# Layer 0 of block 1 by two levels of a Winograd scheme, with the residual in its weights

## The chip, the cores and the metric

The kernel runs on one core of a Trainium2 chip. The metric is the device time of one execution in microseconds (us). TensorE multiplies, VectorE (DVE), ScalarE (ACT) and GpSimd (POOL) do the elementwise work, and SP issues nearly all DMAs; each engine works through its own queue in order.

## The reference

Four layers act on x of 8 sequences x 256 tokens x 1024 features in fp32, each with a residual and each with low-rank adapters (rank 16) that are picked for every sequence by an index. The change concerns the first:

```python
base_out = jnp.einsum('bti,oi->bto', x, W) + b
A = lora_As[adapter_mapping]
Bm = lora_Bs[adapter_mapping]
lora_h = jnp.einsum('bti,bir->btr', x, A)
lora_out = jnp.einsum('btr,bro->bto', lora_h, Bm)
return base_out + lora_out * SCALING        # SCALING = 2
...
x = x + _L0_cond_ref(x, ...)                # residual around layer 0
x = x + _L1_cond_ref(x, ...)                # gate, up, silu(gate) * up, down (F = 2752)
x = x + _L2_cond_ref(x, ...)                # low rank alone
x = x + _L3_cond_ref(x, ...)
```

## The kernel before

**Tiling.** Tokens lie along the free dimension, features along the 128 partitions. The 2048 tokens are two blocks of 1024 (`blk`), each in two halves of 512 (`n`). Layer 0 runs for both blocks first, `layer0(0)` and `layer0(1)`; then for each block gate and up (`gate_up`) and the rest (`down_projection`). What layer 0 gives, x1, is stored to memory (`x1d`) and read again as the residual of layer 1.

**One level and two.** All large products save multiplications by Winograd's form of Strassen's scheme: a 2x2 product of blocks takes seven products of sums of blocks. Layer 0 uses one level: `job(o)` (L894) makes two of the eight output chunks from seven products with 512 columns (`product`, L372), with sums of weights (`sum_w`) and of tokens (`sum_x`) on DVE. Its first quarter in block 0 is `plain` (L865), with no scheme. `with_bias` (L849) evicts a product from PSUM and adds bias and residual x. Gate and up use two levels, `Quads` (L385): 7 steps x 7 blocks, a block being 2 x 2 matmuls with 256 columns in `step` (L464). The outer sums of the tokens, and the inner ones, are made once per block by `prepare_tokens` (L656): DVE and ACT make them from x1, and for each half of the features (`kk`) they are stored to memory (`toks`, 7 places of 7 x 256 columns) and read back for every group of gate and up, two tiles a step (`load_tok`, L419). The weights' outer sums (`outer`, L431) and inner ones (`inner_sums`, L439) are POOL's. A block's products leave PSUM by ACT copies or DVE additions.

**The order of the work.** A list of units (a job, a step) is emitted in turn; each has slots, and between slots things hung on it are emitted: `u.before(k, slot, f)` puts f at a slot of the unit k before it, `u.at(slot, f)` at its own. Light work goes to a queue `beside`, from which each slot takes items until their costs reach the unit's share (1.3 for a layer-0 job, `SHARE` for a step). `need(key)` empties that queue until something is ready. The last block of a step is kept back (`pending`) until slot 2 of the next. The tile framework then orders the instructions of each engine from this, so that a ready load can go ahead of a waiting store.

**Buffers.** Nearly all tiles of 8 KB per partition come from one pool of 22 (`big`, L119), in program order: x, sums, weights, tokens, results.

**Beside the change.** After block 0's jobs, `finished` (L857) stores x1 and puts block 0's token preparation beside block 1's jobs. `SumDown` (L755) loads a slice of the down weights, sums it on POOL and stores the sums (2.1 MB in all each): four of them in block 1's last layer-0 job, four in block 0's groups of gate and up. The first part of gate and up is the remainder (`rest`, L1099), 7 steps of half the width, whose tokens are loaded two units ahead; then five full groups (`job`, L998). A group's low-rank part is four matmuls of 32 rows for each finished result (`expand_gu`, L987).

Of the kernel before, what the change touches and what calls it, by code (L numbers as in the profile page):

```python
# [8 lines left out]
F32 = mybir.dt.float32  # L9
I32 = mybir.dt.int32  # L10
# [7 lines left out]
NB = 8  # L18
S = 256
R = 16  # L20
SLOTS1 = 16
SLOTS2 = 64
TB = 1024
# [31 lines left out]
def kernel(  # L55
# [3 lines left out]
    toks_in: bass.AP,  # L59
    w0: bass.AP,  # L60
    w0a: bass.AP,
    b0: bass.AP,
    a0: bass.AP,
    bb0: bass.AP,
    wgu: list,
    wrem: bass.AP,
    wd2: bass.AP,
# [44 lines left out]
    tpool = ctx.enter_context(tc.tile_pool(name="t", bufs=2))  # L112
# [6 lines left out]
    def big(name):  # L119
        return upool.tile([P, BIG], F32, tag="u", name=name)  # L120

    def bank(pool, name):
        return pool.tile([P, 512], F32, tag=pool.name, name=name)
# [91 lines left out]
    along = const.tile([P, 32], I32, tag="along", name="along")  # L215
    nc.gpsimd.iota(along, pattern=[[1, 32]], base=0, channel_multiplier=0)
    pick = const.tile([P, 32], F32, tag="pick", name="pick")
    nc.vector.tensor_copy(pick, along)
    nc.vector.tensor_scalar(pick, pick, place_f, None, op0=ALU.is_equal)
# [5 lines left out]
    nc.vector.tensor_single_scalar(  # L225
        off_gx[:, :, 1, :], off_gx[:, :, 1, :], 4.0 * R * SLOTS1, op=ALU.add
    )


    def gather(t, table, off):  # L230
# [154 lines left out]
    class Quads:  # L385


        deep = 2
        columns = (1, 0)

        def __init__(self, blk, name, nq, load_raw, done, share):
            self.blk, self.name, self.nq = blk, name, nq
            self.load_raw, self.done = load_raw, done
            self.raw, self.sums, self.tok, self.c = {}, {}, {}, {}
            self.units = []
            for s in range(len(ORDER)):
                u = Unit(f"{name}_{s}", lambda at, s=s: self.step(s, at), share[ORDER[s]])
                u.before(2 if nq == 1 else 1, 0, lambda s=s: self.load_tok(s))
                u.before(1, 1, lambda s=s: self.inner_sums(s))
                self.units.append(u)  # L400
            first = self.units[0]
            first.before(3, 0, lambda: (self.load("B11"), self.load("B12")))
            first.before(2, 0, lambda: self.load("B22"))
            first.before(1, 0, lambda: self.load("B21"))
            self.units[0].at(2, lambda: self.outer("T3", "B22", "B12", "sub"))
            self.units[1].at(3, lambda: self.outer("B12", "B12", "B11", "sub"))
            self.units[2].at(2, lambda: self.outer("B11", "T3", "B11", "add"))
            self.units[4].at(2, lambda: self.outer("B21", "B21", "B11", "sub"))
# [147 lines left out]
    class Down(Quads):  # L556
# [92 lines left out]
            return weights, tokens  # L649


    toks = [
        dram.tile([7, 2, P, 7 * S], F32, tag=f"toks{b}", name=f"toks{b}") for b in range(NBLK)
    ]

    def prepare_tokens(blk, kk, h):  # L656

# [123 lines left out]
    def layer0(blk):  # L781
# [75 lines left out]
        def finished(kk):  # L857
            for n in range(NN):
                nc.sync.dma_start(
                    out=x1d[blk][n, kk], in_=st["x1", n, kk].rearrange("p i c t -> p (i c t)")  # L860
                )
            if blk == 0:
                beside.extend(prepare_tokens(blk, kk, [st["x1", n, kk] for n in range(NN)]))

        def plain(o, at):  # L865

# [27 lines left out]
        def job(o, at):  # L894
# [33 lines left out]
            more(p, 1, pl)  # L928
            at(7)

        for i, o in enumerate((0, 2, 1, 3)):
            if blk == 0 and i == 0:
                u = Unit("0_plain", lambda at, o=o: plain(o, at), 0)
                u.before(1, 0, load_x)
                for c in range(HC):
                    u.before(1, 0, lambda c=c: sum_x(c))
            else:
                u = Unit(f"0_{blk}_{o}", lambda at, o=o: job(o, at), 1.3)
                u.before(1, 0, lambda o=o: load_w(o))
                u.before(1, 3, lambda o=o: sum_w(o))  # L940
                if i == 0:
                    u.before(1, 0, load_x)
                    for c in range(HC):
                        u.before(1, 4 + c // 2, lambda c=c: sum_x(c))
                    u.at(4, first_shrink)
            if i % 2:
                u.at(8, lambda kk=o % 2: finished(kk))
            if blk == 1 and i == 3:
                for c in range(4):
                    w = SumDown(c)  # L950
                    u.at(2 * c - 2 if c else 0, w.load)
                    u.at(2 * c, w.sums)
                    u.at(2 * c + 3, w.store)

    def gate_up(blk):
        st = sts[blk]
# [41 lines left out]
        def job(g):  # L998
# [91 lines left out]

            q = Quads(blk, f"1_{blk}_{g}", 2, raw, done, SHARE)
            q.units[0].before(3, 0, lambda: tables(g))
            if blk == 0 and g < KQ:
                w = SumDown(g + 4)
                q.units[2].at(0, w.load)
                q.units[2].at(5, w.sums)
                q.units[4].at(0, w.store)
# [94 lines left out]
    def down_projection(blk):  # L1192
# [200 lines left out]
        def last_layers():  # L1393


            x2, t, banks = st["x2"], {}, []
            final = blk + 1 == NBLK
            if final:
                spare = big("spare").rearrange("p (j t) -> p j t", j=4)

            def ranks(n):
                rows = slice(64 * n, 64 * n + 64)
                t[n] = tpool.tile([P, 512], F32, tag="t", name=f"t23_{blk}_{n}")
                nc.vector.tensor_mul(t[n][rows], st.pop(("p23", n))[rows], mask[rows])

            def store(o, n):
                at = blk * TB + n * 512

                queue_of = nc.sync if final else nc.scalar
                if final and n == 1 and o in TAIL:  # L1410
                    queue_of = nc.gpsimd
                queue_of.dma_start(out=outT[o * P : (o + 1) * P, at : at + 512], in_=x2[o][n])

            def products(*which):
                pss = []
                for o, n in which:
                    banks.append(None)
                    ps = bank((ps_l, ps_a)[len(banks) % 2], f"p23_{blk}_{o}_{n}")
                    expand(ps, st["a23"], o, t[n], 64 * n, 64 * n + 64, start=True)
                    pss.append(ps)  # L1420
                for (o, n), ps in zip(which, pss):
                    if final and n == 1 and o in TAIL:

                        copy(spare[:, TAIL.index(o)], ps)
                        nc.gpsimd.tensor_add(x2[o][n], x2[o][n], spare[:, TAIL.index(o)])
                        store(o, n)
                        continue
                    nc.vector.tensor_add(x2[o][n], x2[o][n], ps)

                    if final:  # L1430
                        store(o, n)
                    else:
                        beside.append((0.2, lambda o=o, n=n: store(o, n)))

            for c in (HC - 1, NC - 1):
                shrink_half(c, 1)
            shrink_half(HC - 1, 0)
            ranks(1)
            if final:
# [12 lines left out]
            ranks(0)  # L1452
            if not final:
                products((2, 1))
            for o in range(NC - ahead):
                products((o, 0), (o + ahead, 1))
            for o in range(NC - ahead, NC):
                products((o, 0))
# [31 lines left out]
                u.at(6, table_a)  # L1490
        units[-1].at(9, last_layers)

    for blk in range(NBLK):
        layer0(blk)
    for blk in range(NBLK):
        gate_up(blk)
        down_projection(blk)
# [149 lines left out]
```

## Time and profile before

| | |
|---|---|
| time, median of 3 runs | 1804.67 us (1803.13 to 1806.73) |
| the profiled execution | 1805.19 us, span 1803.4 us |
| TensorE | 1790.4 us busy, 99% of the span |
| DVE, ACT, POOL | 1051.5, 298.6, 984.1 us busy |
| DMA | 403.38 MB, 224 GB/s over the span |
| layer 0, block 0 | 0 to 119.3 us, DMA share 0.62 |
| layer 0, block 1 | 119.3 to 227.7 us, DMA share 0.77 |
| remainder of gate and up, block 0 | 227.7 to 273.1 us, DMA share 0.98 |

The span runs from the first to the last instruction; the execution's time has some 1.8 us around it. Lines are named by the engine that worked, the tile written and the line of the kernel (L476 is the matmul of a two-level step, L375 that of a one-level product). fp32 matmuls appear as two instructions each. The DMA share is the part of the time in which the 16 DMA engines were busy, on average.

### The profile page before, as it was taken

The page shows a single profiled execution, that of the slowest core. Times are in us where ns is not written, and L with a number is a line of the kernel's source. Part 1 is how long each engine was busy: PE and PEld are TensorE (multiplying, and loading weights), DVE is VectorE, ACT ScalarE, POOL GpSimd, SP SyncE. Part 2 cuts the span into 40 slices and gives each one's busy share as a digit, 9 for nine tenths or more (in the row PEclk, how much of TensorE's full clock was granted, in tenths as well). Part 3 has the DMA queues.
Part 4 walks back from the last instruction along what each step waited for, and adds up shares of the span by engine and source line. Part 5 has one row for each costly group of instructions (what it writes and reads, how often), then busy time and mean ns, then how long its engine had stood idle before and what let it go on. Part 6 is the DMA issues. An engine that isn't in the chain of part 4 may idle for free.

```text
span 1803.4 us, 20672 instructions
## 1 busy us (share of the span) xinstructions
PE 1790.4 (99%) x7664; PEld 1312.2 (73%) x7664; DVE 1051.5 (58%) x1675; ACT 298.6 (17%) x536; POOL 984.1 (55%) x742
## 2 busy tenths in 40 slices
PE   9999999999999999999999999999999999999998
PEld 4444477888787878788854678787888887888743
DVE  5584255666666666748842464757575758554623
ACT  0121023020202121224210031121212121221000
POOL 6202579685868686344530567676767564443301
PEclk9999999999999999999999999999999999999999
DMA  6476895867676755778831865575848475745302
GB/s 233 172 281 250 273 396 184 304 225 287 215 294 208 298 187 217 260 272 311 316 135 67 307 264 192 176 292 171 296 165 290 166 256 184 255 165 180 110 0 94
DMA packets 119094, 403.38 MB, mean 224 GB/s; under 512 B 11858, under 2 KB 42706, under 8 KB 109522
## 3 DMA queue, kind: packets, MB, share of 16 engines
q1 hardware_dynamic: 108752, 382.24, 58.4%
q0 software_dynamic: 6080, 12.99, 2.3%
q10 hardware_dynamic: 4162, 6.82, 1.2%
q8 instruction: 62, 1.02, 0.2%
q14 instruction: 38, 0.31, 0.0%
HBM read 317.59 MB, written 84.41 MB: 223 GB/s over the span
## 4 chain that ended last, share of the span: by engine, by line
PE 93%; DVE 3%; issue 2%; DMA 1%; POOL 0%; ACT 0%; DVEq 0%; POOLq 0%; ACTq 0%; SPq 0%
PE pa L476 26%; PE pc L476 13%; PE pa_d L476 11%; PE pa L375 10%; PE pb L476 6%; PE pc_d L476 5%; PE pc L375 5%; PE pb_d L476 3%; PE pb L375 2%; PE pl L989 2%; PE pa_r L476 2%; PE pp L875 2%; PE pd L261 1%; PE pc_r L476 1%; DMA w_B<-in_wgu_dram 1%
## 5 line engine op out<-in xcount | busy, mean ns | idle before, releaser
L476 PE MATMUL pa<-tk,sw 128*128 128x256 f32 x1120 | 268.9, 383 | 1.7 <-DVE c_X L507 1.7
L476 PE MATMUL pc<-tk,sw 128*128 128x256 f32 x1120 | 264.9, 379 | 0.3 <-POOL sw L447 0.3
L476 PEld LDWEIGHTS pa<-tk,sw 128*128 128x128 f32 x1120 | 209.0, 190 | 59.9 <-issue 10.6
L476 PEld LDWEIGHTS pc<-tk,sw 128*128 128x128 f32 x1120 | 212.5, 190 | 31.2 <-issue 1.8
L476 PE MATMUL pa<-tk,w_B 128*128 128x256 f32 x960 | 227.8, 380 | 0.0
L476 PEld LDWEIGHTS pa<-tk,w_B 128*128 128x128 f32 x960 | 181.6, 190 | 32.5 <-issue 6.5
L446 POOL TENSOR_TENSOR sw<-w_B 128x512 f32<-128x512 f32 x60 | 76.5, 1275 | 170.8 <-PE pa L476 151.3
L614 POOL TENSOR_TENSOR dx_d<-dw_d 128x1024 f32<-128x1024 f32 x14 | 33.0, 2356 | 164.7 <-PE pa L476 44.3
L476 PE MATMUL pb<-tk,w_B 128*128 128x256 f32 x480 | 113.4, 379 | 0.0
L476 PE MATMUL pa_d<-dh_d,dw_d 128*128 128x256 f32 x448 | 102.2, 379 | 0.0
L476 PE MATMUL pc_d<-dh_d,dw_d 128*128 128x256 f32 x448 | 101.7, 379 | 0.0
L476 PEld LDWEIGHTS pb<-tk,w_B 128*128 128x128 f32 x480 | 91.2, 190 | 12.4
L507 DVE TENSOR_TENSOR c_X<-c_X,pa 128x512 f32<-128x512 f32 x90 | 61.5, 683 | 64.9 <-PE pa L476 64.9
L437 POOL TENSOR_TENSOR w_B<-w_B,w_B 128x1024 f32<-128x1024 f32 x40 | 93.4, 2356 | 2.4 <-PE pa L476 2.4
L476 PEld LDWEIGHTS pa_d<-dh_d,dw_d 128*128 128x128 f32 x448 | 85.0, 190 | 12.4 <-issue 0.8
L476 PEld LDWEIGHTS pc_d<-dh_d,dw_d 128*128 128x128 f32 x448 | 85.0, 190 | 12.4 <-issue 0.8
L448 POOL TENSOR_TENSOR sw<-w_B 128x512 f32<-128x512 f32 x60 | 87.8, 1463 | 0.0
L449 POOL TENSOR_TENSOR sw<-w_B,sw 128x512 f32<-128x512 f32 x60 | 80.6, 1343 | 3.9
L447 POOL TENSOR_TENSOR sw<-sw,w_B 128x512 f32<-128x512 f32 x60 | 76.9, 1282 | 0.0
L286 ACT ACTIVATE c_X<-pa 128x512 f32<-128x512 f32 x30 | 17.7, 591 | 341.1 <-PE pa L476 341.1
L231 POOL DMA_INDIRECT ad<-in_ad_dram,off_a x48 | 46.1, 961 | 31.3 <-PE pd L261 20.9
L375 PE MATMUL pa<-ht,wd 128*128 128x512 f32 x128 | 60.2, 600 | 0.0
(380 smaller groups left out, 3118.1 us busy)
## 6 DMA issues: line engine op xcount, KB each, us to landing
tk<-toks SPq DMA_DIRECT2D x140, 896.0 KB, 6.6
w_B<-in_wgu_dram SPq DMA_DIRECT2D x40, 1024.0 KB, 5.0
tk_r<-toks SPq DMA_DIRECT2D x28, 896.0 KB, 11.0
hk<-c_Z SPq DMA_DIRECT2D x32, 512.0 KB, 4.1
dh_d<-hk SPq DMA_DIRECT2D x14, 1024.0 KB, 8.4
hk<-c_Y SPq DMA_DIRECT2D x24, 512.0 KB, 4.1
x1d<-x SPq DMA_DIRECT2D x8, 1024.0 KB, 6.4
wo<-in_wd_dram SPq DMA_DIRECT2D x8, 1024.0 KB, 7.0
```

The source lines that it names most:

```text
L231: nc.gpsimd.indirect_dma_start(out=t, out_offset=None, in_=table, in_offset=bass.IndirectOffsetOnAxis(ap=off, axis=0),)
L375: nc.tensor.matmul(ps, v[j], m[j], start=start and k == 0, stop=k == len(moving) - 1, skip_group_check=True,)
L437: f(self.raw[out][:, c], self.raw[a][:, c], self.raw[b][:, c])
L446: nc.gpsimd.tensor_add(s1, m21, m22)
L447: nc.gpsimd.tensor_sub(s2, s1, m11)
L448: nc.gpsimd.tensor_sub(s3, m11, m21)
L449: nc.gpsimd.tensor_sub(s4, m12, s2)
L476: nc.tensor.matmul(ps[:, q, :], w(j, q, kk), tok(j, kk), start=start and q == 0 and kk == 0, stop=kk == self.deep - 1, skip_group_check=True,)
L507: nc.vector.tensor_add(view(out, r, k), view(old, r, k), ps)
L614: nc.gpsimd.tensor_sub(s3, a11, a21)
L875: nc.tensor.matmul(pss[j, n], st["w", o][:, i, j // HC], x[c][n], start=i == 0, stop=i == NC - 1,)
L989: nc.tensor.matmul(ps[outs], st["bgu", g][rows, table, n, cols], st["t"][rows, table, n, :], start=True, stop=True, skip_group_check=True,)
```

## The change

- Layer 0 of block 1 becomes `layer0_two(1, ...)`: the class `Quads` of gate and up, seven steps, the two tables being the two halves of the output features. The identity is added to the weights on POOL (`residual`, on the raw quarters B11 and B22), so that the product holds x itself; bias and low-rank part are added to each finished result.
- Its x is loaded in two halves (`load_x`), and its tokens are prepared and stored beside block 0's jobs (`prepare`), with their rank rows (`rank_rows`, `spread_rows`). The share of a job goes from 1.3 to 2.0.
- Block 0's x1 is stored as before, and read again inside the new steps (`load_x1`), where block 0's tokens are now prepared.
- `SumDown`: one in block 0's last job, two in the last two steps, one in each of block 0's five full groups.
- The four loads of raw weights are placed later than in a group of gate and up; one small pool (`tpool`) has one buffer instead of two; masks and offsets are added in the set-up; the host sends W also as quarters (`wq0`) and the adapters' rows in another order (`bx0`).

```diff
@@ Quads @@
+        LOADS = ((("B11", "B12"), 3, 0), (("B22",), 2, 0), (("B21",), 1, 0))
...
-            first.before(3, 0, lambda: (self.load("B11"), self.load("B12")))
-            first.before(2, 0, lambda: self.load("B22"))
-            first.before(1, 0, lambda: self.load("B21"))
+            for keys, k, slot in loads:
+                first.before(k, slot, lambda keys=keys: [self.load(x) for x in keys])
@@ layer0 @@
-            if blk == 0:
-                beside.extend(prepare_tokens(blk, kk, [st["x1", n, kk] for n in range(NN)]))
...
-                u = Unit(f"0_{blk}_{o}", lambda at, o=o: job(o, at), 1.3)
+                u = Unit(f"0_{blk}_{o}", lambda at, o=o: job(o, at), 2.0)
...
-            if blk == 1 and i == 3:
-                for c in range(4):
-                    w = SumDown(c)
...
+    def layer0_two(blk, beside_of):
...
+        def rank_rows(kk):
+            if kk == 0:
+                st["t0"] = big(f"t0_{blk}").rearrange("p (j t) -> p j t", j=4)
+            t = st["t0"]
+            ps = bank(ps_l, f"t0_{blk}_{kk}")
+            for c in range(2):
+                for r in range(4):
+                    k = (r % 2) * HC + 2 * c + kk
+                    shrink_into(ps, r, st["a0"], NC, k, r // 2, h[kk][r // 2][:, r % 2, c], c == 0, c == 1)
+            nc.vector.scalar_tensor_tensor(
+                t[:, 2 + kk], ps, 2.0, mask, op0=ALU.mult, op1=ALU.mult
+            )
+        def spread_rows():
+            t = st["t0"]
+            nc.vector.tensor_add(t[:, 2], t[:, 2], t[:, 3])
+            for n in range(NN):
+                ps, rows = bank(ps_l, f"t0r_{blk}_{n}"), slice(64 * n, 64 * n + 64)
+                nc.tensor.matmul(ps, spread[rows], t[rows, 2], start=True, stop=True)
+                copy(t[:, n], ps)
+        def prepare(kk):
+            beside.append((0.7, lambda: rank_rows(kk)))
+            if kk == 1:
+                beside.append((0.7, spread_rows))
+            beside.extend(prepare_tokens("x", kk, h[kk]))
...
+            def add(r):
+                k = table * HC + r
+                nc.vector.scalar_tensor_tensor(
+                    c[:, r], lo[r], bias[:, k : k + 1], c[:, r], op0=ALU.add, op1=ALU.add
+                )
...
+        loads = (("B11",), 2, 0), (("B21",), 1, 0), (("B12",), 1, 3), (("B22",), 1, 6)
+        q = Quads("x", f"0_{blk}", 2, raw, done, SHARE, loads)
+        def residual(key):
+            for a in range(2):
+                for k in range(2):
+                    c = a * 1024 + k * 512 + a * 256 + k * P
+                    w = q.raw[key][:, c : c + P]
+                    nc.gpsimd.tensor_add(w, w, same)
+        q.units[0].before(1, 0, lambda: residual("B11"))
+        q.units[0].at(1, lambda: residual("B22"))
+        q.units[0].at(0, tables_b)
+        beside_of[0].at(3, tables_a)
+        for kk in range(2):
+            beside_of[2 * kk].at(4 - 4 * kk, lambda kk=kk: load_x(kk))
+            beside_of[kk + 1].at(4 * kk, lambda kk=kk: prepare(kk))
...
+        for kk in range(2):
+            q.units[2 * kk].at(0, lambda kk=kk: load_x1(kk))
+            q.units[2 * kk].at(4, lambda kk=kk: beside.extend(prepare_tokens(0, kk, h["x1", kk])))
+        for c, (u, at) in enumerate(((beside_of[3], 2), (q.units[5], 3), (q.units[6], 2))):
+            w = SumDown(c)
+            u.at(at - 2, w.load)
+            u.at(at, w.sums)
+            u.at(at + 3, w.store)
@@ gate_up @@
-            if blk == 0 and g < KQ:
-                w = SumDown(g + 4)
+            if blk == 0:
+                w = SumDown(g + 3)
...
-    for blk in range(NBLK):
-        layer0(blk)
+    layer0_two(1, layer0(0))
```

More of the change, by code (lines that the diff above doesn't have):

```diff
@@ L20 @@
 R = 16
+SLOTS0 = 32
 SLOTS1 = 16
@@ L61 @@
     w0a: bass.AP,
+    wq0: bass.AP,
     b0: bass.AP,
@@ L64 @@
     bb0: bass.AP,
+    bx0: bass.AP,
     wgu: list,
@@ L111 @@
     bgpool = ctx.enter_context(tc.tile_pool(name="bg", bufs=2))
-    tpool = ctx.enter_context(tc.tile_pool(name="t", bufs=2))
+    tpool = ctx.enter_context(tc.tile_pool(name="t", bufs=1))
     dram = ctx.enter_context(tc.tile_pool(name="dram", bufs=1, space=bass.MemoryType.DRAM))
@@ L214 @@
     nc.vector.tensor_copy(place_f, place)
[L215 to L219, printed above, removed]
+    along = const.tile([P, P], I32, tag="along", name="along")
+    nc.gpsimd.iota(along, pattern=[[1, P]], base=0, channel_multiplier=0)
+    same = const.tile([P, P], F32, tag="same", name="same")
+    nc.vector.tensor_copy(same, along)
+    nc.vector.tensor_scalar(same, same, part_f, None, op0=ALU.is_equal)
+    nc.vector.tensor_single_scalar(along, along, 31, op=ALU.bitwise_and)
+    spread = const.tile([P, P], F32, tag="spread", name="spread")
+    nc.vector.tensor_copy(spread, along)
+    nc.vector.tensor_scalar(spread, spread, place_f, None, op0=ALU.is_equal)
+    pick = spread[:, :32]
     off_gx = const.tile([P, NBLK, 2, NN], I32, tag="off_gx", name="off_gx")
@@ L227 @@
     )
+    off_g0 = const.tile([P, 2, NN], I32, tag="off_g0", name="off_g0")
+    for g in range(2):
+        nc.vector.tensor_scalar(
+            off_g0[:, g], sel_v[:, 0, 1], 4.0 * R, row_f, op0=ALU.mult, op1=ALU.add
+        )
+    nc.vector.tensor_single_scalar(off_g0[:, 1], off_g0[:, 1], 4.0 * R * SLOTS0, op=ALU.add)
     def gather(t, table, off):
@@ L388, with __init__ @@
         deep = 2
+        LOADS = ((("B11", "B12"), 3, 0), (("B22",), 2, 0), (("B21",), 1, 0))
         columns = (1, 0)
-        def __init__(self, blk, name, nq, load_raw, done, share):
+        def __init__(self, blk, name, nq, load_raw, done, share, loads=LOADS):
             self.blk, self.name, self.nq = blk, name, nq
@@ L649, in operands @@
             return weights, tokens
-    toks = [
-        dram.tile([7, 2, P, 7 * S], F32, tag=f"toks{b}", name=f"toks{b}") for b in range(NBLK)
-    ]
+    toks = {
+        b: dram.tile([7, 2, P, 7 * S], F32, tag=f"toks{b}", name=f"toks{b}") for b in (0, 1, "x")
+    }
     def prepare_tokens(blk, kk, h):
@@ L929, in job @@
             at(7)
+        first = len(units)
         for i, o in enumerate((0, 2, 1, 3)):
@@ L947, in layer0, with load_x, tables_a, tables_b @@
                 u.at(8, lambda kk=o % 2: finished(kk))
-            if blk == 1 and i == 3:
-                for c in range(4):
-                    w = SumDown(c)
-                    u.at(2 * c - 2 if c else 0, w.load)
-                    u.at(2 * c, w.sums)
-                    u.at(2 * c + 3, w.store)
+        return units[first:]
+    def layer0_two(blk, beside_of):
+        st = sts[blk]
+        h = {}
+        def load_x(kk):
+            h[kk] = []
+            for n in range(NN):
+                t = big(f"xb_{n}_{kk}").rearrange("p (a t) -> p a t", a=4)
+                at = blk * TB + n * 512
+                nc.sync.dma_start(
+                    out=t,
+                    in_=xT.rearrange("(a k p) t -> p k a t", k=2, p=P)[:, kk, :, at : at + 512],
+                )
+                h[kk].append(t.rearrange("p (i c) t -> p i c t", i=2))
+        def tables_a():
+            st["a0"] = gather_a(a0, 0, blk, f"a0_{blk}")
+        def tables_b():
+            b = st["b0"] = bgpool.tile([P, 2, NN, P], F32, tag="bg", name=f"bx0_{blk}")
+            for table in range(2):
+                for n in range(NN):
+                    gather(b[:, table, n], bx0, off_g0[:, table, n : n + 1])
+        def rank_rows(kk):
[9 more added lines that the diff above has]
+                t[:, 2 + kk], ps, 2.0, mask, op0=ALU.mult, op1=ALU.mult
+            )
+        def spread_rows():
+            t = st["t0"]
+            nc.vector.tensor_add(t[:, 2], t[:, 2], t[:, 3])
+            for n in range(NN):
+                ps, rows = bank(ps_l, f"t0r_{blk}_{n}"), slice(64 * n, 64 * n + 64)
[6 more added lines that the diff above has]
+            beside.extend(prepare_tokens("x", kk, h[kk]))
+        def raw(key, t):
+            nc.sync.dma_start(out=t, in_=wq0[int(key[1]) - 1, int(key[2]) - 1])
+        def done(n, table, c):
+            c = c.rearrange("p q i j t -> p (q i) (j t)")
+            lo = []
+            def lora():
+                for r in range(4):
+                    lo.append(bank(ps_l, f"p0_{blk}_{n}_{table}_{r}"))
+                    rows = slice(32 * r, 32 * r + 32)
+                    nc.tensor.matmul(
+                        lo[r],
+                        st["b0"][rows, table, n],
+                        st["t0"][rows, n],
+                        start=True,
+                        stop=True,
+                        skip_group_check=True,
+                    )
+            def add(r):
+                k = table * HC + r
+                nc.vector.scalar_tensor_tensor(
+                    c[:, r], lo[r], bias[:, k : k + 1], c[:, r], op0=ALU.add, op1=ALU.add
+                )
+            def store():
+                for kk in range(2):
+                    nc.sync.dma_start(
+                        out=x1d[blk][n, kk, :, table * 1024 : (table + 1) * 1024].rearrange(
+                            "p (c t) -> p c t", c=2
+                        ),
+                        in_=c[:, kk::2],
+                    )
+            beside.append((0, lora))
+            for r in range(4):
+                beside.append((0.69, lambda r=r: add(r)))
+            beside.append((1.0, lambda: None))
+            beside.append((0, store))
+        loads = (("B11",), 2, 0), (("B21",), 1, 0), (("B12",), 1, 3), (("B22",), 1, 6)
[13 more added lines that the diff above has]
+            beside_of[kk + 1].at(4 * kk, lambda kk=kk: prepare(kk))
+        def load_x1(kk):
+            h["x1", kk] = []
+            for n in range(NN):
+                t = big(f"xn_{n}_{kk}")
+                nc.sync.dma_start(out=t, in_=x1d[0][n, kk])
+                h["x1", kk].append(t.rearrange("p (i c t) -> p i c t", i=2, c=2))
+        for kk in range(2):
+            q.units[2 * kk].at(0, lambda kk=kk: load_x1(kk))
[5 more added lines that the diff above has]
+            u.at(at + 3, w.store)
@@ L1402, in ranks @@
                 rows = slice(64 * n, 64 * n + 64)
-                t[n] = tpool.tile([P, 512], F32, tag="t", name=f"t23_{blk}_{n}")
+                if not t:
+                    t["all"] = tpool.tile([P, 512], F32, tag="t", name=f"t23_{blk}")
+                t[n] = t["all"]
                 nc.vector.tensor_mul(t[n][rows], st.pop(("p23", n))[rows], mask[rows])
@@ L1607 @@
         "bb0": expands(g["L0_cond_lora_Bs"]),
+        "bx0": np.ascontiguousarray(
+            g["L0_cond_lora_Bs"].reshape(-1, R, 2, D // 2).transpose(2, 0, 1, 3).reshape(-1, P)
+        ),
+        "wq0": quads([g["L0_cond_W"].T[:, : D // 2], g["L0_cond_W"].T[:, D // 2 :]], 2),
         "wgu": [
```

## The prediction

> **What bounds the kernel now.** I read the page's head first, then the chain of waits in order of time, then the busy times by stage.
>
> ```profile
> PE 1790.4 (99%) x7664; PEld 1312.2 (73%) x7664; DVE 1051.5 (58%) x1675; ACT 298.6 (17%) x536; POOL 984.1 (55%) x742
> ```
>
> TensorE is busy 99% of the span. The chain shows what one piece of its work takes:
>
> ```profile
> 122.95 3.44 PE pc L375 x8
> ...
> 133.25 3.60 PE t L261 x32
> ...
> 147.35 0.62 PE pb L276
> 147.98 0.42 PE pb L276
> ...
> 345.42 1.07 PE pl L989 x8
> 346.49 1.93 PE pa L476 x8
> 348.41 1.73 PE pc L476 x8
> ...
> 383.75 1.88 PE pd L261 x16
> ...
> 437.18 1.07 PE pl L989 x8
> ```
>
> Columns are start, length, what. A product of a one-level job (L375, 512 columns) is 8 instructions in 3.43 us, 0.429 each; a block of a two-level step (L476, 256 columns) is 8 in 1.73 us, 0.216 each. Half the columns cost half the time, so a second level pays in full on TensorE. The same place of two groups of gate and up, at 345.42 and 437.18, gives the period of a whole group: 91.76 us.
>
> The table by stage has length, then PE, PEld, DVE, ACT and POOL busy, then clock, DMA share and GB/s. The first two rows are layer 0 of block 1 (its first product to its last expansion) and the stage after it (the remainder of gate and up).
>
> ```profile
> 119.32:227.71 108.39, 108.39 (x289) 46.06 (x289) 43.81 (x70) 11.67 (x22) 35.47 (x33) 1.00 0.77 270
> 227.71:273.13 45.42, 44.82 (x200) 36.87 (x201) 27.34 (x56) 12.57 (x25) 35.00 (x35) 1.00 0.98 398
> ...
> 230.00:270.00 40.00, 39.40 (x177) 32.11 (x176) 22.94 (x49) 10.54 (x22) 31.07 (x31) 1.00 1.00 412
> ```
>
> The changed stage never leaves TensorE idle, and its DMA engines are three quarters busy; right behind it they are full. So the stage is bound by TensorE, its successor almost by both.
>
> **TensorE's share.** Goes: 28 products of 3.43 us (96.1), 16 expansions (four jobs of 0.62 + 3 x 0.42, with 0.2 of refill, 8.4), the rank product (3.60): 108.4, as the stage row says. Comes: 49 blocks and four groups of expansions, which is a group of gate and up without its shrink of the hidden rows, 91.76 - 1.88 - 0.2 = 89.7 us; the 32 rank instructions, now in two halves, 3.8; the two products that spread rank rows over partitions, four instructions, by the L276 rows 1.0. Sum 94.5. **Saved: 13.9 us.** The set-up's few wider constants lie under the first products, before the tokens' sums that begin at 17.8 us; nothing.
>
> **DVE.** Goes: 16 token sums, 16 weight sums, 16 biased evictions. Comes: some 50 additions, most out of PSUM, at 0.68, 16 biased ones at 0.75. The preparations (24 subtractions for each half, about 0.60 from start to start) are now two per block: block 1's beside block 0's jobs, block 0's beside the new steps. In a job of 26 us with 8 slots there is room for both. In a step of 12 us it is tight: 7 own operations (4.2 to 4.8 us) and eight pairs (9.6) make 13.8 to 14.4 us in the two steps that carry a full half. Being some 2 us late twice costs between nothing (an eviction has a block's time to spare, and the additions catch up in the next step) and 5 us. I take nothing beyond the DMA wait below, which falls in the same steps.
>
> **POOL.** 7 x 4 sums of 1.3, four outer differences of 4.7, eight small identity additions (128x128; 0.73 is the 128x256 row, so under that each), twelve down-weight sums of 1.26: about 76 us in 95; hidden, as in a group of gate and up. The extra gathers (4 of 0.95) come early or between.
>
> **DMA is the step I doubt.** Block 1's tokens now go out and come back: 14 pieces of 0.92 MB written (beside block 0, where the trace has 30 idle us) and twelve of them read inside the stage (two earlier): +11.0 MB. Block 0's first half is read again from memory with the second, +4.2; storing the first half's tokens, 6.4 MB, moves from 68-102 us into the stage. Two loads of one-level weights (2.1) and two of the four down-weight sums' transfers (4.2) leave it. Net +15.3 MB. Before, the two stages moved 108.39 x 0.270 + 45.42 x 0.398 = 47.4 MB up to the first full group at 273.1, at most 3.7 of them for later steps: 43.7 needed. After: 59.0 MB, in the time that TensorE would need without waiting, 89.7 + 45.4 = 135.1 us. At the full queue's 412 GB/s that takes 143 us, 8 late; at the best 421, 140 us, 5 late; at 389, the rate where stores of sums and row loads mix (below), 152 us, 17 late.
>
> ```profile
> 100.00:110.00 10.00, 10.00 (x25) 4.43 (x24) 10.00 (x18) 1.75 (x4) 0.00 (x0) 1.00 1.01 389
> ...
> 250.00:260.00 10.00, 10.00 (x47) 8.50 (x46) 8.43 (x19) 0.39 (x1) 7.06 (x9) 1.00 1.02 421
> ...
> 1050.00:1055.00 5.00, 5.00 (x14) 2.46 (x13) 3.42 (x7) 1.82 (x3) 1.04 (x1) 0.72 0.66 269
> ```
>
> The wait comes once, whichever deadline is missed first: what is waited out early is time for the queue to catch up. The first is the fourth step's tokens: behind block 0's stored x1 (2.1), both reloads (4.2), three steps' tokens (5.5) and the first half's stores (6.1 or so), 18 MB and 44 us after the buffers come free at about 122, so at 167 against 160. I take 7 us, between the ends 0 (loads pulled ahead of stores) and 17.
>
> The Trainium skill, "DMA: Bandwidth & Descriptors", section "Where 436 GB/s comes from", says that transfers between HBM and SBUF are held to some 358 GB/s per core; by it, as an estimate, the 59 MB take 165 us, 30 us late, and the change loses 16 us. The rows above show 412 and 421 GB/s for such transfers, so I go by them.
>
> **The clock.** The last row above has a granted clock of 0.72 over 5 us, right behind a TensorE wait of 0.84 us at 1049.6: 1.4 us lost. Other waits as short show none. I add one such loss, 1.4 us; ends 0 and 4. The Trainium skill, "TensorE: Matmul & The Clock Gate", section "Part 1: The HAM clock gate", says that an idle window of about 3.4 us brings the half clock, so a wait of 7 us in one piece would bring it surely, spread waits not.
>
> **Sum.** -13.9 + 7 + 1.4 = -5.5 us. The profiled execution took 1805.19 (span 1803.4 and 1.8 around it), 0.5 over the median of the runs, so 1799.7 against it and **1799.2** against the median 1804.67.
>
> **Rivals.** *All hidden:* stores wait, loads go ahead, and the queue drains beside the first full groups, which move only 207 GB/s. For it: TensorE waited 0.6 us in the full-queue stage of before. It gives 1804.7 - 13.9 = 1790.8.
>
> *Buffers run dry (slower):* the 22 large buffers also hold, in the steps beside block 0's preparation, two reloaded tiles and up to five of sums. Step s+1's tokens can then be loaded only when step s-1's are released, which is in slot 2 of step s (its last block is held back until there), 8.6 us before they are needed. In the full queue a token load took
>
> ```profile
> tk_r<-toks SPq DMA_DIRECT2D x14, 896.0 KB, 11.9
> ...
> w_B<-in_wgu_dram SPq DMA_DIRECT2D x4, 1024.0 KB, 13.9
> ```
>
> from issue to landing, 5.3 late for the weights' 13.9. Four steps so: 21 us, and -13.9 + 21 + 1.4 gives 1813. It decides from a landing of about 12 us on, where four delays eat the gain. Against it: when block 0's jobs end, ten buffers come free at once, and by my count of allocations the second and third loads find room.
>
> *Even:* the queue runs at some 395 GB/s with its stores, 14 us late, and gain and wait cancel: 1804 to 1806. That the arithmetic is not saved at all is excluded by the two L375 and L476 rows.
>
> **How the numbers follow.** The forecast (part of the gain lost to the full queue, 1796 to 1803) 0.45; all or nearly all hidden (1790.8 to 1796) 0.25; even 0.08; buffers run dry (1808 and over) 0.22. About 0.2%, 3.6 us, can be told from no change here, so faster begins at 1801.1: three quarters of the first case, 0.33, and the second, 0.25, make 0.58 faster; the other 0.12 and the even case 0.20 the same; 0.22 slower. The range goes from just under the hidden case, 1790.5, to the buffers' price, 1812.5; costlier starvation and a better end than hidden are left out.
>
> **What would show it.** In the changed profile: blocks of layer 0 of block 1 at 1.73 us, the stage near 95 us plus its waits; DMA share about 1.0 and over 400 GB/s from the first step to the first full group; a few us of TensorE idle released by token or weight loads in the third to fifth step or at the end of the remainder. Wrong: no idle there (hidden), or token loads that SP issues late because a buffer is held by TensorE (buffers), or idle behind DVE in the second and fourth step. A DMA rate under 400 GB/s in these stages would make it too fast by 3 us for each 10 GB/s.

## The result and the profile after

The changed kernel takes 1834.59 us (median of four runs, 1830.33 to 1837.5) against 1805.53 us (1803.13 to 1806.73) before: ratio 1.0159, 95% interval 1.0139 to 1.0178. It is 29 us slower, not 5.5 us faster, and outside the range. The sign is that of the rival of the dry buffers; its mechanism is not what the profile shows.

The head of the page after, and the shares of the chain of waits:

```profile
PE 1793.6 (98%) x7836; PEld 1345.7 (74%) x7836; DVE 1090.3 (60%) x1732; ACT 325.7 (18%) x590; POOL 1047.6 (57%) x789
...
DMA packets 126345, 433.03 MB, mean 237 GB/s; under 512 B 12258, under 2 KB 43106, under 8 KB 116258
...
PE 88%; DMA 5%; DVE 3%; issue 2%; POOL 1%; ACT 1%; SPq 0%; DVEq 0%; POOLq 0%; ACTq 0%
```

TensorE's busy time has gone up by 3 us, although 14 us of its work should have gone, and DMA stands on the chain with 5% (1% before). The page alone says no more: 98% busy looks as healthy as 99%. The table by stage says where (length; PE, PEld, DVE, ACT, POOL busy; clock; DMA share; GB/s):

```profile
60.00:135.29 75.29, 71.64 (x174) 27.34 (x172) 38.18 (x65) 15.20 (x31) 16.31 (x16) 0.95 0.79 288
135.29:302.40 167.11, 144.50 (x626) 114.71 (x625) 102.74 (x171) 42.67 (x83) 109.98 (x94) 0.95 0.99 386
302.40:1830.00 1527.60, 1518.97 (x6873) 1179.50 (x6871) 913.33 (x1402) 260.10 (x465) 880.80 (x633) 1.00 0.60 218
...
80.00:90.00 10.00, 6.34 (x20) 1.34 (x20) 0.00 (x0) 0.60 (x1) 0.00 (x0) 0.73 1.03 364
90.00:100.00 10.00, 10.00 (x28) 3.88 (x22) 8.16 (x13) 0.00 (x0) 6.29 (x8) 0.93 0.50 194
100.00:110.00 10.00, 10.00 (x25) 3.85 (x24) 6.46 (x11) 6.15 (x12) 0.00 (x0) 1.00 0.27 105
140.00:150.00 10.00, 0.74 (x4) 0.31 (x2) 0.00 (x0) 0.00 (x0) 4.13 (x7) 0.80 1.01 413
150.00:160.00 10.00, 5.53 (x14) 4.48 (x15) 5.05 (x8) 5.52 (x11) 10.00 (x6) 0.52 1.01 416
```

The first new step starts at 135.29, the first full group at 302.40; before, the stage that is replaced began at 119.32 and the first full group at 273.13. From there on the two kernels agree (1528.5 and 1530.3 us to the end of the span). All of the loss, and some more, is there at 302.4: 29.3 us. The second row holds most of it: 167.1 us with 144.5 of TensorE, the DMA engines full but for one gap at 235 to 245 us (below, e5). A share a little over 1.00 is possible, since a packet counts whole in the window in which it starts.

TensorE's longest waits, and the chain from the end of the token preparation into the first step (start, length, what):

```profile
PE pa L493 <- ACT c_X L303: 13.7, 1, 13.7
PE t L278 <- DMA xb<-in_xT_dram: 3.7, 2, 3.0
PE pa L493 <- DVE c_X L524: 3.2, 3, 1.5
PE pa_r L493 <- DMA tk_r<-toks: 2.3, 2, 1.3
```

```profile
75.18 13.04 DMA xb<-in_xT_dram
...
88.26 3.46 PE t L278 x12
...
129.41 8.55 DMA toksx<-tt_h_x
...
137.98 15.21 DMA xn<-x1d
...
153.21 0.04 ACT pr_h L303
...
153.75 0.59 ACT c_X L303
...
154.47 3.75 PE pa L493 x8
```

Two places. At 82.7 us the rank rows of block 1's second half wait for that half of x (`xb`), which SP issues behind the stores of block 0's x1. At 140.7 TensorE stops for 13.7 us: it waits for ACT to copy a PSUM tile into `c_X`. ACT was not working. Its timeline (start, length, operation, and in brackets the idle time ahead with its releaser):

```profile
153.21 0.60 ACT L303 ACTIVATE pr_h<-xn 128x512 f32<-128x512 f32 x1 [24.28 <-DMA xn<-x1d]
153.75 0.58 ACT L303 ACTIVATE c_X<-pa 128x512 f32<-128x512 f32 x1
```

The first copy of block 0's token preparation stands ahead of the step's evictions in ACT's queue and waits for block 0's reloaded x1. So an engine 18% busy held TensorE: what stood in front of its evictions waited for a transfer.

**Where 42 us went.** I added up TensorE's timeline by kind, from start to start, from its first instruction at 1.5 us to the first shrink of a full group (at 288.5 us before, 317.0 after). The plan is the prediction's; the last two columns are runs e10 and e11 below, whose queues have room.

| us | before | planned | after | e10 | e11 |
|---|---|---|---|---|---|
| one-level products | 170.0 | 73.9 | 74.3 | 74.5 | 74.7 |
| blocks of two levels | 53.9 | 139.3 | 147.0 | 140.8 | 139.1 |
| expansions of 64 rows | 15.4 | 7.0 | 10.3 | 10.4 | 10.4 |
| rank rows | 7.2 | 7.4 | 11.8 | 8.4 | 8.4 |
| bias rows and spreading | 0 | 5.3 | 7.4 | 5.3 | 5.3 |
| the rest | 39.5 | 39.5 | 38.5 | 38.4 | 39.4 |
| waits | 0.9 | 9.3 | 26.2 | 2.9 | 2.8 |

The planned waits are the forecast's 7 and 1.4 on top of the 0.9 there were. Without the 7 and 1.4 the plan adds up to 273.3, the kernel to 315.5: 42 us more. Of these, 25 are waits, 12 are work that runs slower than in e10, and 5 are work that costs more than planned in e10 too.

### The profile page after: what moved, and what is told of

Read it like the earlier page. It is cut to its first block, busy times and chain, and to the rows that moved or that the text cites. A ratio compares the mean times of both kernels' runs of the same rounds, so it can differ in the third digit from the quotient of the medians.

```text
span 1830.9 us, 21279 instructions
## 1 busy us (share of the span) xinstructions
PE 1793.6 (98%) x7836; PEld 1345.7 (74%) x7836; DVE 1090.3 (60%) x1732; ACT 325.7 (18%) x590; POOL 1047.6 (57%) x789
## 3 DMA queue, kind: packets, MB, share of 16 engines
q1 hardware_dynamic: 116016, 412.13, 61.4%
## 4 chain that ended last, share of the span: by engine, by line
PE 88%; DMA 5%; DVE 3%; issue 2%; POOL 1%; ACT 1%; SPq 0%; DVEq 0%; POOLq 0%; ACTq 0%
PE pa L493 27%; PE pc L493 13%; PE pa_d L493 11%; PE pb L493 6%; PE pa L392 6%; PE pc_d L493 5%; PE pc L392 3%; PE pb_d L493 3%; PE pl L1133 2%; PE pa_r L493 2%; PE pp L891 2%; PE pb L392 1%; PE pd L278 1%; DMA wo<-in_wd_dram 1%; PE pc_r L493 1%
## 5 line engine op out<-in xcount | busy, mean ns | idle before, releaser
L493 PE MATMUL pa<-tk,sw 128*128 128x256 f32 x1232 | 298.0, 385 | 18.0 <-ACT c_X L303 13.7
L493 PE MATMUL pc<-tk,sw 128*128 128x256 f32 x1232 | 292.3, 380 | 0.0
L493 PEld LDWEIGHTS pa<-tk,sw 128*128 128x128 f32 x1232 | 230.7, 191 | 83.0 <-POOL w_T L454 14.9
L493 PEld LDWEIGHTS pc<-tk,sw 128*128 128x128 f32 x1232 | 234.6, 191 | 34.4 <-issue 2.4
L493 PE MATMUL pa<-tk,w_B 128*128 128x256 f32 x1056 | 251.4, 380 | 0.3 <-DVE c_Y L527 0.3
L493 PEld LDWEIGHTS pa<-tk,w_B 128*128 128x128 f32 x1056 | 199.5, 190 | 37.3 <-issue 7.3
L463 POOL TENSOR_TENSOR sw<-w_B 128x512 f32<-128x512 f32 x66 | 84.4, 1279 | 177.0 <-PE pa L493 154.3
L493 PE MATMUL pb<-tk,w_B 128*128 128x256 f32 x528 | 125.0, 379 | 0.0
L493 PEld LDWEIGHTS pb<-tk,w_B 128*128 128x128 f32 x528 | 100.2, 190 | 14.3 <-issue 0.8
L454 POOL TENSOR_TENSOR w_B<-w_B,w_B 128x1024 f32<-128x1024 f32 x44 | 102.8, 2359 | 9.8 <-PE pa L493 9.8
L465 POOL TENSOR_TENSOR sw<-w_B 128x512 f32<-128x512 f32 x66 | 95.1, 1440 | 0.0
L303 ACT ACTIVATE c_X<-pa 128x512 f32<-128x512 f32 x33 | 19.5, 591 | 343.5 <-PE pa L493 343.5
```

The source lines that it names most:

```text
L454: f(self.raw[out][:, c], self.raw[a][:, c], self.raw[b][:, c])
L463: nc.gpsimd.tensor_add(s1, m21, m22)
L465: nc.gpsimd.tensor_sub(s3, m11, m21)
L493: nc.tensor.matmul(ps[:, q, :], w(j, q, kk), tok(j, kk), start=start and q == 0 and kk == 0, stop=kk == self.deep - 1, skip_group_check=True,)
```

## The experiments

Two theories. **H:** single late loads in front of in-order engines are the cause (the second half of x, and the reload in front of ACT); mend these two and the time is back. **Q:** the DMA queue's total between the first new step and the first full group sets when that group starts; a mended wait returns elsewhere. A gain is given in us against the change, as the difference of two ratios times 1805; with intervals of about 0.002 on each ratio, it is good to some 5 us.

**e1, the second half of x loaded earlier.**

```
-            beside_of[2 * kk].at(4 - 4 * kk, lambda kk=kk: load_x(kk))
+            beside_of[0].at(4, lambda kk=kk: load_x(kk))
```

> Both halves of block 1's x are loaded right after block 0's first product, instead of the second half behind block 0's stored x1. The wait of 3.7 us at the second half's rank product and the half clock behind it (3.4 us) should go. Theory H (late loads in front of in-order engines cost the time): 7 us faster than the change, some 1827. Theory Q (the DMA queue's total from the first two-level step to the first full group sets the end): the queue also gets work where it idled at 96 to 111 us, so up to 12 us faster, but only if the stores of the second half move forward too; 1823 to 1829.

1824.06 us, ratio 1.0103 [1.0086, 1.0120]: 10 us less. The wait is gone, and with it a clock at half (0.50 from 84.6 to 91.4 us in the changed kernel, 1.00 from 80 to 90 in e1). The 16 rank instructions of the second half in e1's timeline (start, length, what):

```profile
78.82 1.95 PE L278 MATMUL t<-xb,a 128*32 128x512 f32 x16
```

They take 1.95 us; in the changed kernel the same 16 took 1.93 for four and then 3.46 for twelve. The ACT wait is still 9.4 us. Both theories allow this one: the loads come earlier, and the first step with them (131.3 us instead of 135.3).

**e2, the reload of block 0 one step later.**

```
-            q.units[2 * kk].at(0, lambda kk=kk: load_x1(kk))
-            q.units[2 * kk].at(4, lambda kk=kk: beside.extend(prepare_tokens(0, kk, h["x1", kk])))
+            q.units[1 + kk].at(0, lambda kk=kk: load_x1(kk))
+            q.units[1 + kk].at(4, lambda kk=kk: beside.extend(prepare_tokens(0, kk, h["x1", kk])))
```

> Block 0's first reload and its preparation start one step later, so that ScalarE's first copy out of the reload no longer stands ahead of the first evictions of the first step. Same bytes, same work. Theory H: the wait of 13.7 us and the half clock behind it (some 4.5 us) go, 1816 to 1818. Theory Q: the queue was full during that wait, so the waits come back at the token loads of the next steps and of the remainder; at most 4 us faster, 1830 or more.

1835.14 us, ratio 1.0161 [1.0144, 1.0178]: nothing gained, although the 13.7 us are no longer in the list. TensorE's longest waits in e2 ("issue" is a wait for which the profile names no releaser):

```profile
PE pa L493 <- issue: 6.7, 1, 6.7
PE pc_r L493 <- POOL sw_r L463: 5.2, 1, 5.2
```

Its chain at the same place (start, length, what):

```profile
139.62 16.03 DMA tk<-toksx
...
155.69 2.93 PE pa L493 x6
```

TensorE now gets going at 155.69, when the second step's tokens have landed after 16 us; it had waited for ACT until 154.47. In the one order the reload came late, in the other the tokens, at nearly the same time, though e2 had done six blocks before its stop and the changed kernel three (5.2 us of work). That lead was lost again later: POOL's sums of the remainder's weights (`sw_r`) stood behind the sums of a weight slice, which had waited for its load, and the bias rows came in ten pieces instead of six (12.7 us with the spreading, 7.4 in the changed kernel). H's number for this run is missed; the ACT wait was real, but its time came back elsewhere.

**e3, no token reads after the first step.** The steps of block 1's layer 0 use the first step's tokens again: 11.0 MB fewer.

```
-            self.tok[i] = []
+            if self.blk == "x" and s:
+                self.tok[i] = self.kept
+                return
+            self.tok[i] = self.kept = []
```

> All seven new steps use the tokens loaded for the first one, so 11.0 MB of reads are left out (the result of layer 0 of block 1 is then not that of the reference). Theory Q: 11.0 MB at 0.38 MB/us are 29 us of queue, of which the 32 us of waiting behind the first step lose most: 1808 to 1815. Theory H: the reload that held ScalarE was issued ahead of those reads, so the 13.7 us and the earlier 7 us stay and only the small later waits go: 1820 to 1826.

1821.22 us, ratio 1.0083 [1.0066, 1.0100]: 14 us less. This is H's number (1820 to 1826), not Q's (1808 to 1815): the waits for ACT (9.0) and for x (3.5) stay, as H said, since the reload is issued ahead of the reads that are left out.

**e4, no second preparation.** Block 0's x1 is not reloaded and no tokens are made of it: 17 MB fewer.

```
-            q.units[2 * kk].at(0, lambda kk=kk: load_x1(kk))
-            q.units[2 * kk].at(4, lambda kk=kk: beside.extend(prepare_tokens(0, kk, h["x1", kk])))
...
-            q = Quads(blk, f"1_{blk}_{g}", 2, raw, done, SHARE)
+            q = Quads(blk or "x", f"1_{blk}_{g}", 2, raw, done, SHARE)
...
```

> Block 0's reload, preparation and token stores are left out (17 MB), and gate and up of block 0 read block 1's layer-0 tokens instead (so the output is another). What is left is the new product alone with its loads. If the 13.9 us of TensorE time are really saved, and only the second half's late x (7 us) remains, both theories give 1796 to 1800. A time above 1806 would say that the two-level product itself costs more than the sum said.

1816.81 us, ratio 1.0064 [1.0047, 1.0081]: 17 us less, but still slower than before, so both of my numbers were missed. With 17 MB gone the backlog cannot be all: left are 5.7 us for the second step's tokens, 3.3 for x, a clock of 0.83 (80 to 100 us) and 0.75 (140 to 160), and TensorE work that I had priced too low. That opened a third question, the price of the product itself (e10).

**e5, the three weight slices out of the stretch.** `SumDown` goes to full groups 1 to 3, 6.3 MB that no matmul here waits for.

```
-        for c, (u, at) in enumerate(((beside_of[3], 2), (q.units[5], 3), (q.units[6], 2))):
-            w = SumDown(c)
-            u.at(at - 2, w.load)
-            u.at(at, w.sums)
-            u.at(at + 3, w.store)
...
+                if g in (1, 2, 3):
+                    v = SumDown(g - 1)
+                    q.units[4].at(2, v.load)
+                    q.units[5].at(2, v.sums)
+                    q.units[6].at(2, v.store)
```

> The three slices of down weights (6.3 MB of loads and stores) that are summed in layer 0 move to the second to fourth full groups of gate and up, where the queue is half empty; no other work changes. Theory Q (the DMA queue's total between the first new step and the first full group sets the end): 6.3 MB at 0.38 MB/us are 16 us, some 1818 to 1822. Theory H (late loads in front of in-order engines): the reload comes a few us earlier, since one of the slices is stored right ahead of it, 1829 to 1832.

Ratio 1.0089 [1.0071, 1.0107] (1844.64 against 1828.71 us): 13 us less, which is Q's number (1821 on 1805). No transfer that TensorE waits for was touched, and 6.3 MB at the measured 386 GB/s are 16 us. But more than bytes goes with the slices, as three rows of the changed kernel show (SP's wait, POOL's timeline, the table by stage):

```profile
SPq L793 <- DMA wo<-in_wd_dram: 13.5, 1, 13.5
236.61 1.26 POOL L785 TENSOR_TENSOR wo<-wo 128x512 f32<-128x512 f32 x1 [8.15 <-DMA wo<-in_wd_dram]
235.00:245.00 10.00, 10.00 (x46) 7.43 (x45) 6.41 (x10) 0.00 (x0) 7.99 (x7) 1.00 0.63 224
```

The store of a slice's sums (L793) waits for that slice's load, and in SP's queue the loads of the remainder's weights and tokens stand behind it: SP issues nothing from 223.0 to 237.9 us, and the DMA engines run dry (0.63; some 3.7 us of their time). POOL's sums of the remainder stand behind the slice's in the same way. So H's mechanism, a late load in front of an in-order engine, is in this gain too, on SP and POOL; how much of the 13 us it is was not tried apart. (The slices also leave large buffers free; on that see the rivals below.) On the chip of e5 to e8 the kernel before too took 1828.71 us. The traces of all four show rank products waiting some 14 us longer in the first 80 us, with a clock at half for 20 us; the kernel before was not profiled there. So these four are compared by ratios alone.

**e6, the second half straight from SBUF.** Its x1 tiles are still there when block 0 ends, so they are prepared first, and only the first half is read again: 2.1 MB fewer, and no load ahead of ACT's evictions.

```
-            q.units[2 * kk].at(0, lambda kk=kk: load_x1(kk))
-            q.units[2 * kk].at(4, lambda kk=kk: beside.extend(prepare_tokens(0, kk, h["x1", kk])))
+            def direct():
+                beside.extend(prepare_tokens(0, 1, [sts[0]["x1", n, 1] for n in range(NN)]))
+            if kk == 0:
+                q.units[0].at(4, direct)
+            else:
+                q.units[2].at(0, lambda: load_x1(0))
+                q.units[2].at(4, lambda: beside.extend(prepare_tokens(0, 0, h["x1", 0])))
```

> Block 0's second half is prepared first and straight from its buffers, only the first half is reloaded, two steps later: 2.1 MB less, and ScalarE's first copy waits for no load. Theory H: 13.7 us and the half clock, some 4 us, go: 1816 to 1818. Theory Q: 2.1 MB are 5 us, 1828 to 1830.

Ratio 1.0140 [1.0123, 1.0157]: 3 us less, not 17, and within what two ratios can tell. The wait for ACT is down to 0.9 us, and another stands there instead:

```profile
PE pa L493 <- issue: 5.3, 1, 5.3
```

It is again the first matmul of a step, at 176.83, with 0.95 more for its tokens' load right behind it. H's 17 us are missed a second time, on a change that took away just what H blamed. In the profiled execution the stretch from the first new step to the first full group is 9 us shorter, more than Q's 5 and less than H's 17; some 3 us of that are lost again behind it, where the clock was at half for 10.3 us (3.4 in the changed kernel).

**e7, e1 + e5 + e6 together.**

> The early second half of x, the three weight slices moved out and the kept half together. Theory Q: the gains add, 10 and 16 and 5 us: 1803 to 1806. Theory H: 10 and 17: 1807.

Ratio 1.0024 [1.0010, 1.0038]: 24 us less, and 10 + 13 + 3 is 26; the three hardly overlap. On 1805 that is 1809 us, above both numbers (1803 to 1806 and 1807), H's within the interval.

**e8, e7 with each half of the tokens prepared at the start of its job.**

```
-            beside_of[kk + 1].at(4 * kk, lambda kk=kk: prepare(kk))
+            beside_of[kk + 1].at(0, lambda kk=kk: prepare(kk))
```

> As the three together, and the preparation of the second half of x starts half a job earlier, into the stretch in which the queue idled (some 12 us). Theory Q: up to 5 us faster than the three together, 1798 to 1803. Theory H: no wait stands there any more, so the same time within 2 us.

Ratio 1.0014 [1.0004, 1.0025]: 2 us less than e7, inside both intervals; whether it helps stays open. Q's number is missed (1807.5 on 1805, not 1798 to 1803), and "the same within 2 us", H's, is met. It is the best version of the change that I found, and it doesn't beat the kernel before.

**e9, the change again**, beside e10 and e11.

> The changed kernel once more, beside the two below: 1.5% to 1.7% above the kernel before, as it was. It gives the base for what is measured beside it.

1833.65 against 1804.69 us, ratio 1.0156 [1.0132, 1.0180], as expected.

**e10, the product with the queue relieved**: e4 + e1 + e5, so no second preparation, x early, no weight slices. 

> Block 0's second preparation left out (gate and up of block 0 read block 1's tokens, so the output is another), the second half of x early and the three weight slices moved out: nearly all that the change adds to the queue but its own tokens is gone. If the two-level product with its low-rank part saves the 13.9 us, the time is 10 to 14 us (0.6% to 0.8%) under the kernel before. If the product in its place costs more than the sum said (expansions torn apart, restarts, clock), it is only 0 to 7 us under it.

1798.94 us, ratio 0.9970 [0.9959, 0.9980]: 6 us faster than before. The row of its table by stage where the changed kernel stood still:

```profile
140.00:160.00 20.00, 20.00 (x96) 16.72 (x96) 6.51 (x10) 1.79 (x3) 19.84 (x13) 1.00 0.64 264
```

Some expansions in its TensorE timeline:

```profile
84.58 1.12 PE L293 MATMUL pb<-t_s,b 64*128 64x512 f32 x2
98.15 1.12 PE L293 MATMUL pc<-t_s,b 64*128 64x512 f32 x2
103.66 0.69 PE L293 MATMUL pa<-t_s,b 64*128 64x512 f32 x1
103.67 0.69 PE L293 MATMUL pl<-t_s,b 64*128 64x512 f32 x1
```

The DMA share is 0.64, TensorE works without a gap, and still only 6 of the 13.9 us are there. The last two lines are a pair of 64-row expansions that start together, as all did in the kernel before, and a pair costs 0.42 us there. The first two lines are two in a row for one tile, far from their partners: 1.05 us for two. Four such pieces, 8 of the 24 instructions of block 0's scheme jobs, cost 2.5 us more than as pairs.

**e11, e7 + e3**: the second preparation stays, the token reads go.

> The three edits together (early second half of x, weight slices out, one half kept), and all seven steps use the first step's tokens, so that 11.0 MB of reads are left out too (layer 0 of block 1 is then not that of the reference). Theory Q: the queue has no backlog left, so the waits of the remainder go and the time falls under the kernel before by 3 to 8 us. Theory H: with the early waits gone already, the same as the three together, 2 to 5 us above the kernel before.

1798.71 us, ratio 0.9967 [0.9955, 0.9980]: 6 us faster, as Q said and H did not. Two different ways of relieving the queue end at the same time: that is what the product is worth here. This is the run that separates the theories: against e7 it takes out reads alone, with the early waits gone and the slices out of the way, and by the ratios 10 more us go.

**The stretch from the first new step to the first full group in the runs**, from the table by stage: e1, e2, e3, e5, e6, e7, e11.

```profile
131.27:293.97 162.70, 144.62 (x627) 114.40 (x626) 102.94 (x171) 42.71 (x83) 109.64 (x94) 0.96 0.99 385
136.25:304.43 168.18, 152.85 (x627) 119.13 (x626) 101.61 (x171) 43.25 (x83) 109.79 (x94) 0.93 0.98 384
135.42:287.97 152.55, 141.19 (x627) 115.56 (x625) 103.92 (x171) 42.32 (x82) 114.49 (x96) 0.94 0.93 355
159.93:313.04 153.11, 140.92 (x626) 114.54 (x625) 103.22 (x171) 42.22 (x82) 104.64 (x89) 0.96 0.97 382
159.65:317.59 157.94, 142.74 (x626) 112.72 (x625) 102.39 (x171) 41.96 (x82) 108.72 (x93) 0.98 0.99 389
154.35:298.96 144.61, 140.92 (x627) 113.72 (x626) 101.73 (x170) 40.87 (x79) 102.10 (x85) 0.99 0.96 375
131.06:266.38 135.32, 134.49 (x627) 112.62 (x625) 101.31 (x170) 41.41 (x80) 100.67 (x84) 1.00 0.87 333
```

Length times rate gives the bytes: 64.5 MB in the changed kernel, 62.7 in e1, 64.6 in e2, 58.5 in e5, 61.4 in e6, 54.2 in e7. With the engines nearly full (0.96 to 0.99) the length follows the bytes, and in e2, where only the order changed, both stay. In e3 and e11 the engines have time to spare (0.93, 0.87); e3 still waits for ACT and x, and e11 comes to TensorE's own 135. So Q holds for the stretch as a whole, and H for single waits in it and for what stands ahead of it.

## Why the prediction was wrong

**The step that failed is the DMA step**, and in it the sentence "I take 7 us, between the ends 0 (loads pulled ahead of stores) and 17". The doubt was in the right place, the mechanism (a full queue makes TensorE late) was right, and the sizes were off. The first new step began 11.2 us late, the stretch behind it took 32.0 us more than TensorE needs instead of 7, and 11.2 + 32.0 - 13.9 is the 29.3 us lost.

*The rate.* I took 412 GB/s, a row of the remainder, which mostly reads. The stretch ran at 386 with the engines full, as the row of 389 had shown for sums and row loads that mix. 59.0 MB then take 153 us, not 143: 10 us, of which 3.7 are the gap at 235 to 245 us.

*The volume.* 64.5 MB moved, not 59.0: 14 us more at 386 GB/s. I had taken off 3.7 MB as work for later steps that could wait; in the full queue it did not wait. The other 1.8 MB are a debt from before: from 90 to 110 us the DMA engines were half and then three quarters idle (shares 0.50 and 0.27), because the second half of x had landed at 88 us and what was to be stored of it was still to be made. e1 bears this out: with that half early, the stretch moves 62.7 MB, which is 59.0 and the 3.7. 167.1 us against the 135.1 that TensorE would need: 32 late, where the sum at 412 GB/s had 8. The 135.1 itself was right: e11 takes 135.3.

*The late start.* The first step was to begin at 119.32 + 3.8 + 1.0 = 124.1 and began at 135.3. The second half's load, SP's queue and the half clock behind them had no term in the sum; e1 shows that the load's place is worth 10 us in all, 4 of them at this start. In e10 the first step still begins at 130.0: the other 6 us are block 0's own jobs, mostly torn expansions and short waits. I had counted what is issued and not what it is issued behind.

**"The wait comes once"** was right as a rule and gave the wrong answer. e2 and e6 show just this: what isn't waited at one place is for the most part lost at the next. But it holds for the total, so the total had to be right.

**TensorE's share** (13.9) was the term I did not doubt, and some 6 were there (e10, e11). The blocks cost what the rows said (139.1 in e11 against 139.3; the 1.7 more in e10 go with a clock of 0.50 from 261.5 to 264.9 us), and half the columns do cost half the time. Of the 6.7 us that e11 is above the plan, 3.4 are expansions, priced as pairs when a third of block 0's were torn apart (2.5 of the 3.4), 1.9 short waits, 1.0 rank rows and 0.8 products. The three terms listed under 108.4 add up to 108.1; 108.4 is the stage's row.

**The clock**: 1.4 us taken. In the table above, blocks, rank rows and bias rows cost 12 us more after the change than in e10; some 2 of these are not the clock, but bias rows in six pieces instead of four. Up to 302.4 us the granted clock was at half in three pieces, the first two at the two waits (rows of the table by stage):

```profile
84.60:91.40 6.80, 5.07 (x16) 0.82 (x16) 0.00 (x0) 0.60 (x1) 0.00 (x0) 0.50 1.03 410
154.47:159.70 5.23, 5.23 (x12) 4.18 (x13) 4.64 (x8) 3.96 (x8) 5.23 (x4) 0.50 1.01 416
296.20:299.60 3.40, 3.40 (x10) 2.68 (x9) 2.42 (x5) 1.22 (x2) 0.00 (x0) 0.50 1.01 416
```

TensorE worked 13.7 us in them, so my estimate of the loss to the clock is half of that, some 7 us where I had 1.4; e10 lost 1.7 in the same way. The remaining 4 to 5 of the 12 I did not separate.

**DVE and POOL** at nothing was nearly right: no single wait for either is above 1.5 us, but the additions into c_X come to 3.2 (1.7 before) and POOL's sums of the remainder to 3.6 (0.3 before). In e10 POOL's are 1.1, and part of the 3.6 is the slice's late load (e5).

**The rivals.** Dry buffers (1808 and over) got the side, and its condition was met: the token loads took 13 to 15 us to land. But loads held back for want of buffers would leave the DMA engines idle, and they were busy for 0.99 of the 167 us, with the one gap behind a store. SP's token loads did wait for TensorE to give buffers back, 14.3 us in six waits, but before the change these were 19.5 us in nine, where TensorE waited 0.6. A run with more buffers was not made, so a share of theirs in the order of the transfers stays open. All hidden was refuted by the first row of the waits, "even" by a queue 32 us late where it had 14.

**The pages.** The Trainium skill, "DMA: Bandwidth & Descriptors", section "Where 436 GB/s comes from", gave 30 us late for the 59 MB, close to the measured 32, yet not by its reason: single rows stand at 413 and 416 GB/s, above 358, and the lateness came of volume and mixture. The Trainium skill, "TensorE: Matmul & The Clock Gate", section "Part 1: The HAM clock gate", says that an idle window brings the half clock, and the long stop shows it: idle from 140.7 us, a clock of 0.50 from 146.0, and still 0.50 when TensorE worked again (154.47 to 159.70). The 0.50 from 296.2 us came without such a window; there the measurement decides.

## What to carry to other kernels

Between two deadlines, add up every byte that will move, what is "for later" included, and divide by the rate of a stage with the same mixture, not of the best one; a stage whose DMA share is already near 1.0 behind the change has no room to give. If a wait in a full queue is removed and the time stays, compare bytes and length of the whole stretch: where both stayed (e2), the queue's total is the likely cause, and moving bytes that nobody waits for helps more (6.3 MB gave 13 us) than moving the instruction that waits. Look at the issuing engine's queue as well: a store that waits for its own data holds up the loads behind it (13.5 us on SP). A copy that waits for a load blocks everything behind it on its engine, PSUM evictions too, so look for what stands ahead of them even on an engine that is 18% busy.

## What the runs showed of the hardware

- Short stops did not always bring the half clock, and it came once without a long one. In the changed kernel 260 to 270 us has 3.0 us without TensorE, in several pieces, at a clock of 1.00; 290 to 300 has 0.5 us without it and 0.83.
- Two 64-row matmuls of 512 columns into different PSUM tiles start within 0.01 us of each other and take 0.42 us for the pair (0.53 at the head of a run of pairs); two in a row for the same tile, away from their partners, take 1.05. The same with 32 rows: eight in one piece take 1.07 us, two that were split off take 1.05 as well (L1033, at 215.14 us).
- At a share of 1.00 the DMA engines moved 412 GB/s over 40 us in the remainder before, and at 0.99 they moved 386 over 167 us here, where stores of sums are mixed in and ten of the us ran at 224. Which of the transfers is the slow one was not tried apart.
